# Mixture-of-experts routing in 16-bit floats, with the gates stored behind the feature rows

## The chip, the cores and the metric

The kernel runs on one core of one Trainium2 chip. The metric is the device time of one execution in microseconds (us), and the kernel before is given by the median of three runs: 1179.99 us (1179.2 to 1181.08). The profile is of one further execution, which took 1180.66 us; the span from its first to its last instruction is 1178.6 us.

Engines are named as the profile names them: PE (TensorE, matrix products into PSUM; PEld is its loading of the stationary operand), DVE (VectorE), ACT (ScalarE), POOL (GpSimd), SP (SyncE, which here only issues transfers).

## The reference

The reference is one block of a graph transformer on 1250 nodes with 768 features, all in fp32. Its last part, which the change touches, is a layer of eight experts of which each node uses two:

```python
xn = _layernorm(x)
x = x + gnn(xn, edges) + linear_attention(xn)
xt = _layernorm(x)                                # 1250 x 768
gate = xt @ Wg + bg                               # 1250 x 8
scores, idx = jax.lax.top_k(gate, 2)
h = gelu(einsum('td,edh->eth', xt, W1) + b1)      # 768 -> 384, each expert
y = einsum('eth,ehd->etd', h, W2) + b2            # 384 -> 768
comb = sum(one_hot(idx, 8) * scores[..., None])
out = x + einsum('te,etd->td', comb, y)
```

The score by which an expert's output is multiplied is the raw gate value of that node for that expert.

## The kernel before, in words

**Stages.** Until about 595 us the kernel builds the graph's adjacency and runs the two graph layers and the key side of the attention. From about 613 us it multiplies out the update weights, and from about 630 us a loop over ten tiles of 125 nodes (L768) makes the block's output and routes each tile. From about 937 us the experts run, one after the other; what they compute is added onto `out` in HBM.

**One tile of the loop.** `query(t + 1)` (L742 to 765) computes the next tile's attention queries: products `mm` on PE (L751), then on DVE L753 to L762, among them the normalisation `qy`, then transposes of `qy` on PE and their copy `qT` on ACT (L319 to L321, a helper called `turn`). Then 24 products `po` (L781) add the update of this tile, `xt` (the input rows, loaded by L772) gets its sums on DVE (L783, L786), four products `u` (L792) and their sums (L794) complete it. It is written to `out` (L797), normalised into `xl` (L800), and `xl` is written to a scratch matrix `xl_d` in HBM (L802). Transposed, it gives the gate: products `g` (L807), and `gate` on DVE (L810).

**Routing.** DVE ranks the eight gates of each node (L817 to L821), marks first and second choice (`kth`, L825) and their sum `sel`. Two products `g` at L830 count, for each expert, the nodes that chose it up to this one: a triangle of ones `tri` times `sel`, and a square of ones times the counts `cum` of the tiles before. From that each node's place in its expert's list follows (`at`, `two`, `both`; L833 to L845): a slot number and a row number. An expert's list has ten slots of 128 nodes, eight lists make NV = 80 slots. For each of the two choices, `hot` (L849) is a one-hot row of 128 by row number, `put` (L852) is a one-hot row of 80 by slot, once times the node's number and once times its gate, and the product `inv` (L854) of the two adds them into a 128 x 160 table in PSUM: node numbers in the first 80 columns, gates in the last 80. All these are fp32. After the last tile the two halves become `idx` (L858, L859) and `gs` (L861), and L866 to L895 work out which slots beyond the first three of an expert are in use; L867 uses `ones` and `cum` once more.

**Experts.** `gather` (L904) fetches three slots of an expert: for each, POOL issues an indirect load (L909) of 128 rows of `xl_d` by a column of `idx` into `xg`, which PE transposes into `px` (L912) and DVE copies to `xsT` (L915). `hidden` makes the first layer (L926), `give` the second (L938); DVE adds the bias (L941), ACT multiplies by a column of `gs` (L942), and POOL issues an indirect accumulating write to `out` (L943). The gather of the next expert is written between `hidden` and `give` of this one. A ninth round with one slot, `other` (L959), takes its slot and expert from values computed at run time.

**Order of the work.** Each engine runs its instructions in one fixed order. That order is not the source's: it is drawn up when the program is built, from the source's order and from what waits for what. In the trace, products of `query` for a later tile and `po` of the next tile stand on PE between the routing products of this tile. All loads and stores except the indirect ones go through SP's queue in SP's order; the indirect ones go through POOL's. Waits between engines are semaphores that are placed with the order.

Of the kernel before, what the change touches and what calls it, by code (L numbers as in the profile page):

```python
# [27 lines left out]
F32 = mybir.dt.float32  # L28
F16 = mybir.dt.float16
# [5 lines left out]
ALU = mybir.AluOpType  # L35
# [3 lines left out]
N, D = 1250, 768  # L39
PT, NT = 125, 10  # L40
# [3 lines left out]
NE, FF = 8, 384  # L44
# [9 lines left out]
NJ = -(-N // 128)  # L54
FIX = 3
NV = NE * NJ
# [13 lines left out]
def gps_block(ctx: ExitStack, tc: tile.TileContext, x, src, dst, norm_g, norm_b, W1, a_src1, a_dst1,  # L70
              b1, W2, a_src2, a_dst2, b2, Wu, bu, Wq, bq, Wk, bk, Wv, bv, Wo, bo, Wg, bg, fW1, fb1,
              fW2, fb2, out):
    nc = tc.nc
# [10 lines left out]
    dram = ctx.enter_context(tc.tile_pool(name="dram", bufs=1, space=bass.MemoryType.DRAM))  # L84
# [3 lines left out]
    def token_rows(t):  # L88
        return [(slice(0, 112), t), (slice(112, PT), t)]
# [40 lines left out]

    xl_d = dram.tile([N + 128, D], F32)

# [39 lines left out]
    rows = fl.tile([KC, 128], F32)  # L172
# [27 lines left out]
    with tc.tile_pool(name="eps", bufs=4, space=PSUM) as eps_p:  # L200
# [4 lines left out]
        for k in (1, 0):  # L205
            nc.vector.memset(ends[k][:, T:], float(NO_NODE))
            for r0, r1 in blocks128:
# [6 lines left out]
                if k == 1:  # L214
# [3 lines left out]
                                                   op0=ALU.is_lt, op1=ALU.mult)  # L218
# [21 lines left out]
    with tc.If(nc.values_load(odd[0:1, 0:1], min_val=0, max_val=1) > 0), ExitStack() as es:  # L240
# [9 lines left out]
        for j in range(NT):  # L250
# [21 lines left out]
            for g0 in range(0, NT, 4):  # L272
                n = min(4, NT - g0)
# [266 lines left out]
    with tc.tile_pool(name="wp", bufs=3) as wp, tc.tile_pool(name="rb", bufs=1) as rb:  # L540
# [20 lines left out]
        at = 2 * (C2 + 1)  # L561
# [123 lines left out]

    zero = fp.tile([128, D], F32)
    nc.gpsimd.memset(zero, 0.0)
    nc.sync.dma_start(xl_d[N:], zero)
    nc.sync.dma_start(out[N:], zero)
# [4 lines left out]
    gs = fp.tile([128, NV + 1], F32)  # L694
    fb1T = fp.tile([128, FC, NE], F32)
# [3 lines left out]
    with ExitStack() as rs:  # L699
# [6 lines left out]

        def numbers(shape, pattern, base, mult, name):
            t = rp.tile(shape, F32, name=name)
# [7 lines left out]
        nc.vector.tensor_scalar(upto, upto, 0.0, None, op0=ALU.is_ge)  # L716
        row128 = numbers([PT, 128], [[1, 128]], 0, 0, "row128")
        steps = numbers([128, NE, NJ - FIX], [[0, NE], [128, NJ - FIX]], 128 * FIX, 0, "steps")
        slot_row = numbers([PT, NV], [[1, NV]], 0, 0, "slot_row")
        base = numbers([PT, NE], [[128 * NJ, NE]], -1, 0, "base")  # L720
# [4 lines left out]
        nobody = numbers([128, 1], [[0, 1]], N + 1, 1, "nobody")  # L725
        ones = rp.tile([PT, 128], F32)
        nc.gpsimd.memset(ones, 1.0)
        tri = rp.tile([PT, 128], F32)
        nc.gpsimd.affine_select(tri, ones, pattern=[[1, 128]], compare_op=ALU.is_ge, fill=0.0,
                                base=0, channel_multiplier=-1)  # L730
        nc.gpsimd.tensor_copy(idx[:, NV:], nobody)
        nc.vector.tensor_scalar(idx[:, NV:], nobody, -1.0, None, op0=ALU.add)
        nc.gpsimd.memset(gs[:, NV:], 0.0)
        for f in range(FC):
# [3 lines left out]

        cum = rp.tile([PT, NT + 1, NE], F32)
        nc.vector.memset(cum[:, 0], 0.0)  # L740
        inv = g_p.tile([128, 2, NV], F32, name="inv", bufs=1)
        def query(t):  # L742
# [25 lines left out]
        for t in range(NT):  # L768
# [29 lines left out]

            xl = rl.tile([PT, D], F32, name="xl")
            normalise(xl, xt)  # L800
            for p, tt in token_rows(t):
                nc.sync.dma_start(xlr[p, tt], xl[p])  # L802
            xT = rl.tile([128, KC, PT], F32, name="xT")
            turn(xT, xl, u_p, "u", nc.scalar.copy)
            pg = g_p.tile([128, 2 * NV], F32, name="g")
            for c in range(KC):
                nc.tensor.matmul(pg[:PT, :NE], xT[:, c], Wg_sb[:, c], start=c == 0,  # L807
                                 stop=c == KC - 1)
            gate = rl.tile([PT, NE], F32, name="gate")
            nc.vector.tensor_add(gate, pg[:PT, :NE], bg_b)  # L810

            gt = rl.tile([PT, NE, NE], F32, name="gt")
# [9 lines left out]
            kth = rl.tile([PT, 2, NE], F32, name="kth")  # L822
            sel = rl.tile([PT, NE], F32, name="sel")
            for k in range(2):
# [8 lines left out]
            nc.vector.tensor_add(at, pp[:PT, :NE], base)  # L833
            two = rl.tile([PT, 2, 2, NE], F32, name="two")
            for i, a in enumerate((at, gate)):
                nc.vector.tensor_mul(two[:, i], kth, a[:, None, :].to_broadcast([PT, 2, NE]))
            both = rl.tile([PT, 2, 2], F32, name="both")
            nc.vector.tensor_reduce(both, two, AX.X, ALU.add)
            b_i = rl.tile([PT, 2], I32, name="b_i")
            nc.vector.tensor_copy(b_i, both[:, 0])  # L840
            s_i = rl.tile([PT, 2, 2], I32, name="s_i")
# [5 lines left out]
            for k in range(2):  # L847
                hot = rl.tile([PT, 128], F32, name="hot")
                nc.vector.tensor_scalar(hot, row128, s_f[:, 1, k:k + 1], None, op0=ALU.is_equal)  # L849
                put = rl.tile([PT, 2, NV], F32, name="put")  # L850
                for i, v in enumerate((node1[:, t:t + 1], both[:, 1, k:k + 1])):
                    nc.vector.tensor_scalar(put[:, i], slot_row, s_f[:, 0, k:k + 1], v,  # L852
                                            op0=ALU.is_equal, op1=ALU.mult)
                nc.tensor.matmul(inv.rearrange("p a s -> p (a s)"), hot,  # L854
                                 put.rearrange("p a s -> p (a s)"), start=k == 0 and t == 0,
                                 stop=k == 1 and t == NT - 1)
        free = rp.tile([128, NV], F32)
        nc.vector.tensor_scalar(free, inv[:, 0], 0.0, nobody, op0=ALU.is_equal, op1=ALU.mult)  # L858
        nc.vector.scalar_tensor_tensor(idx[:, :NV], inv[:, 0], -1.0, free, op0=ALU.add,  # L859
                                       op1=ALU.add)  # L860
        nc.vector.tensor_copy(gs[:, :NV], inv[:, 1])  # L861
        for e in range(1, 4):
# [40 lines left out]

    def gather(rows):  # L904

        xT = sp.tile([128, KC, FIX * 128], F32, name="xsT")
        for j, r in enumerate(rows):
# [9 lines left out]
        return xT  # L917

    def hidden(w, xT, n, bias):
# [26 lines left out]
    def fixed(e):  # L946
        return [(idx[:, v:v + 1], gs[:, v:v + 1]) for v in range(e * NJ, e * NJ + FIX)]

    xT = gather([r for r, _ in fixed(0)])
    for e in range(NE):  # L950
        hT = hidden(ring[e], xT, FIX, fb1T[:, :, e:e + 1])
        if e + 1 < NE:
            xT = gather([r for r, _ in fixed(e + 1)])
        for j, (rows, gates) in enumerate(fixed(e)):
            give(ring[e], hT, j, rows, gates)
        if e + 4 < NE:
            ring.append(expert(fW1[e + 4], fW2[e + 4], fb2[e + 4]))

    def other(k):  # L959

        ve = nc.values_load(v_row[0:1, k:k + 1], min_val=0, max_val=NV,
                            engines=[mybir.EngineType.DVE])
        ee = nc.values_load(e_row[0:1, k:k + 1], min_val=0, max_val=NE - 1,
                            engines=[mybir.EngineType.DVE, mybir.EngineType.SP])
        rows = sp.tile([128, 1], I32, name="rows")
        nc.vector.tensor_copy(rows, idx[:, bass.ds(ve, 1)])
        gates = sp.tile([128, 1], F32, name="gates")
        nc.vector.tensor_copy(gates, gs[:, bass.ds(ve, 1)])
# [4 lines left out]
        hT = hidden(w, gather([rows]), 1, bias)  # L973
        give(w, hT, 0, rows, gates)

# [40 lines left out]
```

## Time and profile before

| what | value |
|---|---|
| median of three runs | 1179.99 us |
| profiled execution, its span | 1180.66 us, 1178.6 us |
| PE busy | 1077.8 us (91%), 4583 instructions |
| DVE busy | 669.1 us (57%), 1366 instructions |
| ACT busy | 358.1 us (30%) |
| POOL busy | 76.3 us (6%) |
| granted PE clock, mean | 0.971 of full |
| g L830, 10 tiles | 40 records of 0.17 to 0.38 us |
| inv L854, 10 tiles | 40 records, 9.1 us busy |
| put L852 | 40 instructions, 12.6 us busy |

Busy time is the sum of the instructions of an engine. PE overlaps one product with the next and with the loads, so its busy share says little of how fast it works; what counts is the chain, which is followed back from the last instruction to what released each step. An fp32 product shows as two records on PE (x4 for two products). "Idle before" with an engine and a line names what a waiting instruction was released by. In lists by time, rows of one kind that follow each other are put together as x2, x4 and so on.

### The profile page before, as it was taken

To read this page: it belongs to the slowest core of one execution; us is meant where nothing else is said; L and a number is where in the kernel's file an instruction comes from. 1 tells how busy PE (TensorE), PEld (TensorE's weight loads), DVE (VectorE), ACT (ScalarE), POOL (GpSimd) and SP (SyncE) were. 2 spreads that over 40 slices of the span, in tenths; PEclk is the share of its full clock that TensorE was granted. 3 is DMA by queue.
4 is the path that set the end of the run, shared out by engine and by line. 5 is a ranking of instruction groups with operands and counts; after the bars stand their busy time and mean duration, and the time that the engine had idled before them with its cause. 6 is when DMAs were issued, how large, how long until landed. Compare 5 with 4: busy or idle time off the path is not lost.

```text
span 1178.6 us, 12106 instructions
## 1 busy us (share of the span) xinstructions
PE 1077.8 (91%) x4583; PEld 723.6 (61%) x4583; DVE 669.1 (57%) x1366; ACT 358.1 (30%) x527; POOL 76.3 (6%) x100
## 2 busy tenths in 40 slices
PE   2599998999999999988989999999999589999993
PEld 2586655578788878544545666666666356666652
DVE  6866666669696966687922555555555422222210
ACT  2131114373737373373712211111111011111111
POOL 1000000000000000000000000000000122322321
PEclk9999998999999999989989999999999789999997
DMA  5014000000000001000083111111123537777533
GB/s 156 27 51 163 16 25 1 1 1 1 1 1 1 1 1 53 1 0 1 1 319 103 40 40 40 40 40 40 39 65 106 191 91 188 200 209 219 121 56 54
DMA packets 33282, 79.62 MB, mean 68 GB/s; under 512 B 5258, under 2 KB 13020, under 8 KB 33208
## 3 DMA queue, kind: packets, MB, share of 16 engines
q1 hardware_dynamic: 27608, 59.02, 15.2%
q0 software_dynamic: 5600, 19.66, 8.4%
q8 instruction: 40, 0.66, 0.2%
q14 instruction: 34, 0.28, 0.1%
HBM read 60.37 MB, written 18.30 MB: 67 GB/s over the span
## 4 chain that ended last, share of the span: by engine, by line
PE 70%; DVE 20%; DMA 5%; issue 2%; ACT 2%; POOL 1%; DVEq 0%; SPq 0%; POOLq 0%; ACTq 0%
PE po L781 13%; PE ph L926 8%; PE py L938 7%; PE mm L430 7%; PE mm L607 7%; PE mm L751 7%; DVE scr L515 6%; DVE w L535 5%; DVE w L536 5%; PE ag L548 3%; PE ag L569 2%; PE u L792 2%; PE px L912 2%; PE mm L405 2%; DMA w<-in_L_gnn_Wu_dram 2%
## 5 line engine op out<-in xcount | busy, mean ns | idle before, releaser
L548 PE MATMUL ag<-kept,w 125*125 125x198 f32 x800 | 137.4, 333 | 5.1 <-DVE w L536 4.9
L548 PEld LDWEIGHTS ag<-kept,w 125*125 125x125 f32 x800 | 133.5, 188 | 9.0 <-DVE w L536 9.0
L926 PE MATMUL ph<-xsT,w 128*128 128x384 f32 (+1 forms) x324 | 100.6, 470 | 1.8 <-DVE xsT L915 1.8
L938 PE MATMUL py<-w,hT 128*128 128x384 f32 x300 | 100.6, 486 | 0.0
L430 PE MATMUL mm<-Wg,xnT 128*125 128x400 f32 x240 | 91.8, 520 | 1.0 <-DVE xnT L321 0.6
L607 PE MATMUL mm<-Wv_sb,xnT 128*125 128x384 f32 x240 | 85.7, 489 | 4.8 <-DVE kvacc L627 4.8
L535 DVE TENSOR_TENSOR w<-v,w 125x1250 f32<-125x1250 f32 x60 | 86.3, 1453 | 6.6 <-ACT w L533 5.9
L515 DVE CUSTOM_DVE_ANT_0 scr<-ss_row,mask 125x1250 bf16<-125x1250 f32 x60 | 87.2, 1453 | 0.5 <-ACT ss_row L506 0.2
L781 PE MATMUL po<-w,xnT 128*125 128x384 f32 x240 | 84.8, 496 | 2.6 <-DMA w<-in_L_gnn_Wu_dram 2.6
L536 DVE SCALAR_TENSOR_TENSOR w<-w,AT 125x1250 f32<-125x1250 f32 x60 | 86.4, 1455 | 0.4
L926 PEld LDWEIGHTS ph<-xsT,w 128*128 128x128 f32 x324 | 59.8, 193 | 41.4 <-DVE xsT L915 2.4
L607 PE MATMUL mm<-Wk_sb,xnT 128*125 128x384 f32 x240 | 84.4, 486 | 0.0
L534 ACT ACTIVATE v<-dn_row,sl 125x1250 f32<-125x1250 f32 x60 | 79.3, 1333 | 16.9 <-DVE w L535 16.4
L751 PE MATMUL mm<-w,xnT 128*125 128x384 f32 x240 | 84.2, 489 | 0.0
L915 DVE COPY xsT<-px 128x384 f32<-128x384 f32 x50 | 25.5, 552 | 99.2 <-PE px L912 77.3
L781 PE MATMUL po<-w,qT 128*125 128x384 f32 x240 | 80.8, 486 | 0.0
L938 PEld LDWEIGHTS py<-w,hT 128*128 128x128 f32 x300 | 55.3, 190 | 33.9
L941 DVE TENSOR_TENSOR ys<-py,wb 128x768 f32<-128x768 f32 x25 | 23.9, 958 | 74.0 <-PE py L938 45.5
L781 PEld LDWEIGHTS po<-w,xnT 128*125 128x125 f32 x240 | 44.2, 190 | 30.1 <-DMA w<-in_L_gnn_Wu_dram 2.8
L781 PEld LDWEIGHTS po<-w,qT 128*125 128x125 f32 x240 | 44.2, 188 | 29.4
L607 PEld LDWEIGHTS mm<-Wv_sb,xnT 128*125 128x125 f32 x240 | 42.4, 187 | 31.1 <-DVE kvacc L627 6.9
L751 PEld LDWEIGHTS mm<-w,xnT 128*125 128x125 f32 x240 | 43.6, 188 | 27.6 <-ACT qT L321 0.2
(274 smaller groups left out, 1415.6 us busy)
## 6 DMA issues: line engine op xcount, KB each, us to landing
w<-in_L_ffn_W_dram SPq DMA_DIRECT2D x18, 1152.0 KB
xt<-in_x_dram SPq DMA_DIRECT2D x20, 336.0 KB
wb<-in_L_ffn_b_dram SPq DMA_DIRECT2D x9, 384.0 KB
out_dram<-xt SPq DMA_DIRECT2D x10, 336.0 KB
xl_d<-xl SPq DMA_DIRECT2D x10, 336.0 KB
W_sb<-in_L_gnn_W_dram SPq DMA_DIRECT2D x1, 2304.0 KB
Wk_sb<-in_L_mix_Wk_dram SPq DMA_DIRECT2D x1, 2304.0 KB
Wv_sb<-in_L_mix_Wv_dram SPq DMA_DIRECT2D x1, 2304.0 KB
```

Source lines behind the costliest of these rows:

```text
L430: nc.tensor.matmul(ps[:PT, :2 * (CG + 2)], xnT[:, c, t * PT:(t + 1) * PT], Wg1[:, c, 2 * k:2 * k + 2].rearrange("p h c -> p (h c)"), start ...
L515: nc.vector.tensor_tensor_reduce(scr, ss_row, mask[:, t], 1.0, 0.0, ALU.mult, ALU.max, top[:, t:t + 1])
L534: nc.scalar.activation(v, dn_row, AF.Exp, bias=sl[:, st:st + 1])
L535: nc.vector.tensor_tensor(w, v, w, op=ALU.max)
L536: nc.vector.scalar_tensor_tensor(w, w, 2.0, AT[:, st, :N], op0=ALU.min, op1=ALU.mult)
L548: nc.tensor.matmul(ag[:, t // 2, o:o + CG], w[:, t * PT:(t + 1) * PT], gw[:, st, hd], start=st == 0 and t % 2 == 0, stop=st == NT - 1, ski ...
L607: nc.tensor.matmul(ps[:PT, :384], xnT[:, c, t * PT:(t + 1) * PT], w[:, c, half], start=c == 0, stop=c == KC - 1)
L751: nc.tensor.matmul(ps[:PT, :384], xnT[:, c, tk], Wq_sb[:, c, half], start=c == 0, stop=c == KC - 1)
L781: nc.tensor.matmul(po[k][:, :384], l, r[:, k * 384:(k + 1) * 384], start=i == 0, stop=i == len(parts) - 1)
L915: nc.vector.tensor_copy(xT[:, 3 * a:3 * a + 3, j * 128:(j + 1) * 128], px[:, a, :384].rearrange("p (b n) -> p b n", b=3))
L926: nc.tensor.matmul(ph[:, :n * 128], w[0][:, o:o + 128], xT[:, c, :n * 128], start=c == 0, stop=c == KC - 1)
L938: nc.tensor.matmul(py[:, k, :384], hT[:, f, j * 128:(j + 1) * 128], w[:, o:o + 384], start=f == 0, stop=f == FC - 1)
```

## The change

Two things are changed.

First, types. `row128`, `slot_row`, `ones`, `tri`, `cum`, `sel`, `hot` and `put` become 16-bit floats. Their values are 0, 1, slot and row numbers, node numbers and counts up to 1250, all whole numbers that a 16-bit float holds exactly up to 2048. Products still add up in fp32 in PSUM.

Second, the gates take another way. A row of `xl_d` is 776 instead of 768 numbers long: behind the features stand the node's eight gates. `gate` is now the end of the tile `xl`, and two more transfers per tile (112 and 13 rows of 32 bytes) write it. The gates' half of `two`, `both`, `put` and `inv` goes, and with it `gs`. A gather brings the eight gates along, and one more DVE copy per slot takes the expert's column out of `xg` into `gates`; for the computed slot the column is given by a register.

The diff, cut to its core:

```diff
-    xl_d = dram.tile([N + 128, D], F32)
+    xl_d = dram.tile([N + 128, D + NE], F32)
...
-        row128 = numbers([PT, 128], [[1, 128]], 0, 0, "row128")
+        row128 = numbers([PT, 128], [[1, 128]], 0, 0, "row128", F16)
-        slot_row = numbers([PT, NV], [[1, NV]], 0, 0, "slot_row")
+        slot_row = numbers([PT, NV], [[1, NV]], 0, 0, "slot_row", F16)
-        ones = rp.tile([PT, 128], F32)
+        ones = rp.tile([PT, 128], F16)
-        tri = rp.tile([PT, 128], F32)
+        tri = rp.tile([PT, 128], F16)
...
-        cum = rp.tile([PT, NT + 1, NE], F32)
+        cum = rp.tile([PT, NT + 1, NE], F16)
-        inv = g_p.tile([128, 2, NV], F32, name="inv", bufs=1)
+        inv = g_p.tile([128, NV], F32, name="inv", bufs=1)
...
-            xl = rl.tile([PT, D], F32, name="xl")
-            normalise(xl, xt)
+            xl = rl.tile([PT, D + NE], F32, name="xl")
+            normalise(xl[:, :D], xt)
             for p, tt in token_rows(t):
-                nc.sync.dma_start(xlr[p, tt], xl[p])
+                nc.sync.dma_start(xlr[p, tt, :D], xl[p, :D])
...
-            gate = rl.tile([PT, NE], F32, name="gate")
+            gate = xl[:, D:]
             nc.vector.tensor_add(gate, pg[:PT, :NE], bg_b)
+            for p, tt in token_rows(t):
+                nc.sync.dma_start(xlr[p, tt, D:], gate[p])
...
-            sel = rl.tile([PT, NE], F32, name="sel")
+            sel = rl.tile([PT, NE], F16, name="sel")
...
-            two = rl.tile([PT, 2, 2, NE], F32, name="two")
-            for i, a in enumerate((at, gate)):
-                nc.vector.tensor_mul(two[:, i], kth, a[:, None, :].to_broadcast([PT, 2, NE]))
+            two = rl.tile([PT, 2, NE], F32, name="two")
+            nc.vector.tensor_mul(two, kth, at[:, None, :].to_broadcast([PT, 2, NE]))
...
-                hot = rl.tile([PT, 128], F32, name="hot")
+                hot = rl.tile([PT, 128], F16, name="hot")
                 nc.vector.tensor_scalar(hot, row128, s_f[:, 1, k:k + 1], None, op0=ALU.is_equal)
-                put = rl.tile([PT, 2, NV], F32, name="put")
-                for i, v in enumerate((node1[:, t:t + 1], both[:, 1, k:k + 1])):
-                    nc.vector.tensor_scalar(put[:, i], slot_row, s_f[:, 0, k:k + 1], v,
-                                            op0=ALU.is_equal, op1=ALU.mult)
+                put = rl.tile([PT, NV], F16, name="put")
+                nc.vector.tensor_scalar(put, slot_row, s_f[:, 0, k:k + 1], node1[:, t:t + 1],
+                                        op0=ALU.is_equal, op1=ALU.mult)
...
-        nc.vector.tensor_copy(gs[:, :NV], inv[:, 1])
...
-            xg = sp.tile([128, D], F32, name="xg", bufs=3)
+            xg = sp.tile([128, D + NE], F32, name="xg", bufs=3)
...
+            at = slice(D + e, D + e + 1) if isinstance(e, int) else bass.ds(e + D, 1)
+            nc.vector.tensor_copy(gates[:, j:j + 1], xg[:, at])
```

`give` then multiplies by a column of `gates`. `hidden` is renamed `inner` and is otherwise the same; `zero`, which fills the rows of `xl_d` behind the last node, is as wide as the new rows.

More of the change, by code (lines that the diff above doesn't have):

```diff
@@ L684, in gps_block @@
             nc.scalar.copy(Wo_sb[:, c, half], ps[:, :384])
-    zero = fp.tile([128, D], F32)
+    zero = fp.tile([128, D + NE], F32)
     nc.gpsimd.memset(zero, 0.0)
     nc.sync.dma_start(xl_d[N:], zero)
-    nc.sync.dma_start(out[N:], zero)
+    nc.sync.dma_start(out[N:], zero[:, :D])
     ring = [expert(fW1[0], fW2[0], fb2[0])]
@@ L693, in gps_block @@
     idx = fp.tile([128, NV + 1], I32)
-    gs = fp.tile([128, NV + 1], F32)
     fb1T = fp.tile([128, FC, NE], F32)
@@ L705, in gps_block, with numbers @@
         u_p = rs.enter_context(tc.tile_pool(name="u_p", bufs=2, space=PSUM))
-        def numbers(shape, pattern, base, mult, name):
-            t = rp.tile(shape, F32, name=name)
+        def numbers(shape, pattern, base, mult, name, dt=F32):
+            t = rp.tile(shape, dt, name=name)
             nc.gpsimd.iota(t, pattern=pattern, base=base, channel_multiplier=mult,
@@ L732, in gps_block @@
         nc.vector.tensor_scalar(idx[:, NV:], nobody, -1.0, None, op0=ALU.add)
-        nc.gpsimd.memset(gs[:, NV:], 0.0)
         for f in range(FC):
@@ L833, in gps_block @@
             nc.vector.tensor_add(at, pp[:PT, :NE], base)
-            two = rl.tile([PT, 2, 2, NE], F32, name="two")
-            for i, a in enumerate((at, gate)):
-                nc.vector.tensor_mul(two[:, i], kth, a[:, None, :].to_broadcast([PT, 2, NE]))
-            both = rl.tile([PT, 2, 2], F32, name="both")
+            two = rl.tile([PT, 2, NE], F32, name="two")
+            nc.vector.tensor_mul(two, kth, at[:, None, :].to_broadcast([PT, 2, NE]))
+            both = rl.tile([PT, 2], F32, name="both")
             nc.vector.tensor_reduce(both, two, AX.X, ALU.add)
             b_i = rl.tile([PT, 2], I32, name="b_i")
-            nc.vector.tensor_copy(b_i, both[:, 0])
+            nc.vector.tensor_copy(b_i, both)
             s_i = rl.tile([PT, 2, 2], I32, name="s_i")
@@ L847, in gps_block @@
             for k in range(2):
-                hot = rl.tile([PT, 128], F32, name="hot")
+                hot = rl.tile([PT, 128], F16, name="hot")
                 nc.vector.tensor_scalar(hot, row128, s_f[:, 1, k:k + 1], None, op0=ALU.is_equal)
-                put = rl.tile([PT, 2, NV], F32, name="put")
-                for i, v in enumerate((node1[:, t:t + 1], both[:, 1, k:k + 1])):
-                    nc.vector.tensor_scalar(put[:, i], slot_row, s_f[:, 0, k:k + 1], v,
-                                            op0=ALU.is_equal, op1=ALU.mult)
-                nc.tensor.matmul(inv.rearrange("p a s -> p (a s)"), hot,
-                                 put.rearrange("p a s -> p (a s)"), start=k == 0 and t == 0,
+                put = rl.tile([PT, NV], F16, name="put")
+                nc.vector.tensor_scalar(put, slot_row, s_f[:, 0, k:k + 1], node1[:, t:t + 1],
+                                        op0=ALU.is_equal, op1=ALU.mult)
+                nc.tensor.matmul(inv, hot, put, start=k == 0 and t == 0,
                                  stop=k == 1 and t == NT - 1)
         free = rp.tile([128, NV], F32)
-        nc.vector.tensor_scalar(free, inv[:, 0], 0.0, nobody, op0=ALU.is_equal, op1=ALU.mult)
-        nc.vector.scalar_tensor_tensor(idx[:, :NV], inv[:, 0], -1.0, free, op0=ALU.add,
-                                       op1=ALU.add)
-        nc.vector.tensor_copy(gs[:, :NV], inv[:, 1])
+        nc.vector.tensor_scalar(free, inv, 0.0, nobody, op0=ALU.is_equal, op1=ALU.mult)
+        nc.vector.scalar_tensor_tensor(idx[:, :NV], inv, -1.0, free, op0=ALU.add, op1=ALU.add)
         for e in range(1, 4):
@@ L902, in gps_block, with gather @@
     y_p = ctx.enter_context(tc.tile_pool(name="y_p", bufs=2, space=PSUM))
-    def gather(rows):
+    def gather(rows, e):
         xT = sp.tile([128, KC, FIX * 128], F32, name="xsT")
+        gates = sp.tile([128, FIX], F32, name="gates")
         for j, r in enumerate(rows):
-            xg = sp.tile([128, D], F32, name="xg", bufs=3)
+            xg = sp.tile([128, D + NE], F32, name="xg", bufs=3)
             nc.gpsimd.indirect_dma_start(xg, None, xl_d, bass.IndirectOffsetOnAxis(r, 0))
@@ L916, in gather, with inner @@
                                       px[:, a, :384].rearrange("p (b n) -> p b n", b=3))
-        return xT
-    def hidden(w, xT, n, bias):
+            at = slice(D + e, D + e + 1) if isinstance(e, int) else bass.ds(e + D, 1)
+            nc.vector.tensor_copy(gates[:, j:j + 1], xg[:, at])
+        return xT, gates
+    def inner(w, xT, n, bias):
         hT = sp.tile([128, FC, FIX * 128], F32, name="hT")
@@ L946, in fixed @@
     def fixed(e):
-        return [(idx[:, v:v + 1], gs[:, v:v + 1]) for v in range(e * NJ, e * NJ + FIX)]
-    xT = gather([r for r, _ in fixed(0)])
+        return [idx[:, v:v + 1] for v in range(e * NJ, e * NJ + FIX)]
+    ahead = gather(fixed(0), 0)
     for e in range(NE):
-        hT = hidden(ring[e], xT, FIX, fb1T[:, :, e:e + 1])
+        xT, gates = ahead
+        hT = inner(ring[e], xT, FIX, fb1T[:, :, e:e + 1])
         if e + 1 < NE:
-            xT = gather([r for r, _ in fixed(e + 1)])
-        for j, (rows, gates) in enumerate(fixed(e)):
-            give(ring[e], hT, j, rows, gates)
+            ahead = gather(fixed(e + 1), e + 1)
+        for j, rows in enumerate(fixed(e)):
+            give(ring[e], hT, j, rows, gates[:, j:j + 1])
         if e + 4 < NE:
@@ L966, in other @@
         nc.vector.tensor_copy(rows, idx[:, bass.ds(ve, 1)])
-        gates = sp.tile([128, 1], F32, name="gates")
-        nc.vector.tensor_copy(gates, gs[:, bass.ds(ve, 1)])
         bias = sp.tile([128, FC, 1], F32, name="bias")
@@ L972, in other @@
                    fW2[bass.ds(ee, 1)].rearrange("o d f -> (o d) f"), fb2[bass.ds(ee, 1)])
-        hT = hidden(w, gather([rows]), 1, bias)
-        give(w, hT, 0, rows, gates)
+        xT, gates = gather([rows], ee)
+        hT = inner(w, xT, 1, bias)
+        give(w, hT, 0, rows, gates[:, :1])
     def others(k):
```

## The prediction

> **What bounds the kernel now.** I read the page first (1180.66 us for the profiled execution, 1178.6 us of it span), then the chain in order of time over one steady token tile, then the timeline of VectorE and SyncE in that tile, then the chain of the last tile. The routing work sits in the loop over ten token tiles (roughly 672 to 937 us). In it the chain is TensorE without a gap:
>
> ```profile
> 851.97 0.35 PE g L830 x4
> 852.31 2.68 PE po L781 x8
> 854.99 0.67 PE inv L854 x4
> 855.66 4.52 PE po L781 x14
> 860.18 0.65 PE mm L319 x6
> 860.83 7.10 PE po L781 x22
> ```
>
> Columns: start, length, engine, tile, line, count. The next tile's g L830 comes 29.53 us later (881.84 - 852.31 between the same po groups in the whole chain), and table rows by stage show TensorE busy in all of it. So what is cut from TensorE here shortens the tile, unless VectorE then sets the pace. VectorE is close to that (start, length, engine, line, operation, tiles):
>
> ```profile
> 852.35 0.17 DVE L833 TENSOR_TENSOR at<-g,base 125x8 f32<-125x8 f32 x1 [0.25 <-PE g L830]
> ...
> 854.09 0.32 DVE L852 TENSOR_SCALAR put<-slot_row,s_f,both 125x80 f32<-125x80 f32 x1
> 854.33 0.28 DVE L849 TENSOR_SCALAR hot<-row,s_f 125x128 f32<-125x128 f32 x1
> ...
> 854.75 0.31 DVE L852 TENSOR_SCALAR put<-slot_row,s_f,both 125x80 f32<-125x80 f32 x1
> 854.98 0.95 DVE L756 SCALAR_TENSOR_TENSOR qy<-qy,qe 125x768 f32<-125x768 f32 x1
> ...
> 858.95 0.96 DVE L762 TENSOR_TENSOR qy<-qy,den 125x768 f32<-125x768 f32 x1
> ```
>
> From `at` to the end of L762 (859.91) VectorE has no pause, and the transposes of qy (L319) start on TensorE at 860.01: their weight load started at 859.97, so VectorE is 0.04 us from being the one that ends last. Both must be shortened for the tile to shrink. After the last tile nothing covers the routing:
>
> ```profile
> 930.49 1.04 PE g L830 x4
> ...
> 931.77 0.61 PE g L867 x2
> ...
> 933.79 0.47 DVE put L852 x2
> ...
> 934.30 1.57 PE inv L854 x4
> ...
> 935.90 0.30 DVE free L858
> ...
> 937.47 4.06 DMA xg<-xl_d,idx
> ```
>
> Here every step delays the first gather and so all eight experts, which then keep TensorE busy for 190.87 of the 190.90 us from 949.1 to 1140.
>
> **What the Trainium skill says.** "FP8 and Floating Point Precision", section TensorE Precision Notes: true fp32 takes four passes through the array. The trace agrees: an fp32 product of 384 columns is two records that take 0.65 us of the chain (L751 x2), 1.7 ns a column. "TensorE: Matmul & The Clock Gate", section on weight-path perf modes: a load of 128 weights that aren't fp32 can be about twice as fast. The trace has fp32 loads of 186 to 192 ns and bf16 ones of 138 ns with 125 columns, none with 128 and 16 bits. "VectorE: DVE Perf Modes", perf-mode tier table: tensor_scalar from SBUF runs at 4 elements a cycle in 16 bits, 2 in fp32; no row before shows the 16-bit form here. "DMA: Bandwidth & Descriptors", Specifications: writes under 512 B are read-modify-write; no such write to HBM is in this stage of the trace before.
>
> **The change, part by part.**
>
> *TensorE, a steady tile.* The fp32 pairs become single records, 16-bit, of 8 and 80 columns. The nearest row is the 16-bit product with a fresh weight load at full clock: eight ec L350 take 0.47 us, ten pm L465 take 0.58 us of the chain, so 0.058 us each. g L830: 2 x 0.058 = 0.12 instead of 0.35, saves 0.23. inv L854: 0.12 instead of 0.67 (of which about 0.1 us is waiting for the second put), saves 0.55. Sum 0.78 us. Bounds: 0.85 if the 128-column load is quicker, 0.70 if a change of type costs some 0.04 us at each group.
>
> *VectorE, a steady tile.* Two puts go, 0.23 us each by their starts (854.09 to 854.33): 0.46. g L830 ends 0.23 earlier. hot and put in 16 bits: 128 columns at 4 instead of 2 a cycle is 32 cycles, 33 ns, an estimate by the VectorE page; the starts are 0.2 us apart at any size here, so 0 to 0.11 us in four instructions; I take 0.05. The gate product L836 goes too (0.08 us between starts), outside this stretch. Sum 0.74, and with the 0.04 in hand VectorE allows 0.78. The tile thus shrinks by 0.77 us, and both engines stay level. Nine tiles: **6.9 us**.
>
> *The last tile*, at half clock, with cold 16-bit products at 0.107 us apart (ten pm L465 in 1.07 us) and 315 ns from start to end (longest of that row). g L830: 0.04 + 0.107 + 0.315 = 0.46 instead of 1.06 to the start of `at`: 0.60. g L867, for which VectorE waits before it goes on: 0.36 instead of 0.64: 0.28. Two puts: 0.46. From the last put (934.90) to `free` (935.90) 1.0 us becomes about 0.5, because begin, late, mine and place (until 935.38) are then last: 0.50. Sum 1.84 us. The copy of gs comes after idx, and saves nothing there.
>
> *The first gather.* It is issued 0.99 us after idx is written (936.24 + 0.24). The named releaser is the transpose L894, which moves up as well. Rows grow from 3072 to 3104 bytes: 1% of 4.06 us at least, 0.4 us if odd row starts cost 10%; I take 0.1. If the wider buffer falls on a tile that the second L894 still reads, up to 0.75 us more. Net of the tail: **1.7 us**.
>
> *Gate writes*, two per tile of 112 and 13 rows with 32 bytes each. Nobody on an engine waits for them but the gathers. SyncE's row of the tile:
>
> ```profile
> 846.26 0.76 SPq L802 DMA_DIRECT2D xl_d<-xl  x2
> 847.13 0.92 SPq L772 DMA_DIRECT2D xt<-in_x_dram  x2
> ```
>
> The gate is ready at 849.49. Placed after L772, its writes cost nothing: SyncE is then idle until 871.84. Placed before it, in source order, the loads of the next xt start at 849.5 + 0.8 = 850.3 instead of 847.13; their traffic ended by 851 before (DMA share 0.17 from 850 to 851, zero after), so it would end at about 854 with the small writes. L783 reads xt at 855.85, now some 0.75 earlier, 855.1: hidden with 1 us to spare, on VectorE before L757, L759 and the qy chain. Without that cover each microsecond late is one per tile. The last tile's gate is ready at 928.79; SyncE issued its last weight load at 925.56 and the DMA share is 0.05 from 932 to 933, so the writes land by about 933 even behind those weights. The gather would go at 937.47 - 1.84 = 935.6: 2.6 us of cover.
>
> *Expert phase.* 24 copies of one column (gates to xg), about 0.15 us each by the old copy L968, 3.7 us of VectorE, which is busy 42 of 191 us there and waits mostly for py. They read xg after the gather, as the transposes do, so they add no earlier wait; a buffer of xg comes free about 1 us later, against 25 us until its next use. The copy of the computed slot moves from before its gather to after it, ahead of nothing that ends last: the end is the row of accumulating writes to out from 1146 on. Cost 0. Iotas, memsets and the zero store of 3104-byte rows lie behind the weight loads at 594 to 613 us: 0.
>
> **Sum:** 6.9 + 1.7 = 8.6 us; the profiled execution goes from 1180.66 to 1172.1, the span to 1170.0, and the median of three runs, 1179.99, to **1171.4**.
>
> **Rivals.** (A) *The order of instructions is drawn anew.* The trace shows that each engine's order is not the source's: products of later tiles stand between routing's. Eight po records (2.68 us) now cover VectorE's stretch from g L830 to the second put (2.9 us). Shorter routing may leave six (1.93 us) against about 2.35: 0.4 us of waiting per tile, 3.6 in nine. For: cover and stretch are matched to 0.2 us today. Against: the stretch shrinks by as much as a po pair. Time 1180.0 - 5.0 = 1175.0. (B) *Hidden anyway:* if qy's chain starts from something that the change doesn't shorten (exp L755, done by 852.9), only the tail is won: 1178.3. Against: L756 follows the last put at once, and exp was done 2 us before. (C) *Slower: the gate write stands before the next xt load in SyncE's queue and makes xt late.* VectorE stops before L783, and with it qy, its transposes and po. It needs xt to land after 855.1; to lose the gain it must land 0.95 us later than that on all nine tiles, and with 1.4 us later the kernel takes 1180.0 + 12.6 - 8.6 = 1184.0. For: source order puts it there. Against: my estimate of 854. (D) *The change doesn't do what it says:* if one 16-bit product took as long as its fp32 pair, g L830 would save nothing, and inv only the width and the wait for the second put, about 0.2 per tile, with 1 us at the end: 1177.2. Against: the 0.058 us rows.
>
> **How the numbers follow.** My forecast (1169.5 to 1173.5) 0.60; A and D (1173.5 to 1177.6) 0.22; B 0.08, within 0.2% (2.4 us, about what a measurement of this kernel can tell from no change); C 0.10. The range 1168.8 to 1177.6 holds the first two, 0.82; its low end is 0.85 a tile and 2.5 us at the end, with something over. Faster 0.82, same 0.08, slower 0.10.
>
> **What would show it.** Right: tile period near 28.76 us; g L830 and inv L854 at two records each and about 0.12 us of the chain; no TensorE idle before L854 or L319; inv to first gather shorter, with idx near 1.8 us sooner after the last gate; experts unchanged. Wrong: VectorE idle before L783 until an xt landing (C), TensorE waiting for put (A) or for qy L762, the first gather waiting for a gate write, or 16-bit records more than 0.1 us apart at full clock (D).

## The result, and the profile after

The changed kernel takes 1167.35 us (median of 6 runs, 1160.77 to 1169.57) against 1180.09 us (6 runs, 1176.61 to 1182.83) for the kernel before: ratio 0.9892, 95% interval 0.9872 to 0.9912. That is faster, as forecast, but by 12.7 us instead of 8.6, and 1.45 us below the low end of the range. Two repetitions gave 0.9899 (0.9879 to 0.9918) and 0.9912 (0.9893 to 0.9932).

The profiled execution after took 1167.08 us, its span 1165.0 us. Between landmarks that both traces have, in us:

| stage | before | after | difference |
|---|---|---|---|
| start to the first po product | 612.97 | 610.79 | -2.18 |
| to the first count product g (L830, now L831) | 62.18 | 61.92 | -0.26 |
| to the ninth one: eight tiles | 234.46 | 228.21 | -6.25 |
| to the tenth one | 20.88 | 19.83 | -1.05 |
| to the first gather | 6.98 | 4.48 | -2.50 |
| to the first ph product | 11.66 | 11.72 | +0.06 |
| to the eighth expert's first py product | 190.95 | 190.66 | -0.29 |
| to the last accumulating write to `out` | 26.59 | 25.70 | -0.89 |
| to the end | 11.94 | 11.71 | -0.23 |

So 9.8 us come from the loop and the steps behind it (the rows of the eight tiles, the tenth count product and the first gather), and 3.8 us from stages in which the change does nothing or nearly nothing. Both parts need an explanation.

**A steady tile.** The chain of waits of the kernel after (start us, length us, engine, line, count), the same stretch as in the prediction:

```profile
844.82 0.03 PE g L831 x2
844.85 2.04 PE po L780 x6
846.89 0.04 PE inv L853
846.93 0.72 PE po L780 x2
847.65 0.04 PE inv L853
847.68 4.59 PE po L780 x14
852.27 0.64 PE mm L319 x6
```

From the start of g to the end of the mm group there were 8.87 us before (0.35 + 2.68 + 0.67 + 4.52 + 0.65), and there are 8.09 now. TensorE still has no gap, and the period is 28.77 us instead of 29.53. The two `inv` products have come apart: the first now stands after six po records (three products), as rival A said, but it doesn't wait there, and the second stands two records later. VectorE in the same tile (timeline: start, length, engine, line, operation, tiles):

```profile
844.89 0.17 DVE L834 TENSOR_TENSOR at<-g,base 125x8 f32<-125x8 f32 x1
...
846.73 0.30 DVE L851 TENSOR_SCALAR put<-slot_row,s_f,node 125x80 f16<-125x80 f16 x1
...
850.91 0.96 DVE L761 TENSOR_TENSOR qy<-qy,den 125x768 f32<-125x768 f32 x1
```

It ends at 851.87, and the weight load of the transposes of qy starts 0.05 us later, as before (859.91 and 859.97). But the product behind that load follows at 852.11, 0.19 us after it, where it followed within 0.05 us before: TensorE is still busy with po then. So VectorE shrank by a little more than TensorE, and has some 0.14 us in hand.

**Behind the last tile.** The chain after:

```profile
920.76 0.21 PE g L831 x2
...
920.99 0.18 DVE at L834
...
921.21 0.18 PE g L863
...
923.13 0.22 DVE put L851
...
923.40 0.24 PE inv L853
...
923.66 0.30 DVE free L856
...
925.24 4.12 DMA xg<-xl_d,idx
```

What the products gain is larger than the prediction had it: g to `at` takes 0.23 us instead of 1.06. The weight loads (PEld) say why. Before, the loads of `tri` and `ones` belong to their fp32 product and start with it, when `sel` is there; after, they are instructions of their own. First before, then after:

```profile
930.49 0.50 PEld L830 LDWEIGHTS g<-sel,tri 125*128 125x128 f32 x2 [2.00 <-DVE sel L826]
```

```profile
918.50 0.29 PEld L831 LDWEIGHTS <-tri 125*128 125x128 f16 x1
...
920.78 0.10 PEld L863 LDWEIGHTS <-ones 125*128 125x128 f16 x1
```

`tri` is loaded 2.26 us before its product at 920.76, and the `ones` of the total at 920.78, 0.43 us before theirs at 921.21. The Trainium skill, "TensorE: Matmul & The Clock Gate", section Step-by-step: what each phase is for, says that TensorE pulls weight loads ahead of products that are under way. This trace agrees for the 16-bit products; the fp32 loads of `tri` and of the total's `ones` in the kernel before wait with theirs (930.49 and 931.77).

**The gates' writes.** SyncE's queue after:

```profile
842.37 0.75 SPq L811 DMA_DIRECT2D xl_d<-xl  x2
843.23 0.76 SPq L771 DMA_DIRECT2D xt<-in_x_dram  x2
```

They stand ahead of the next load of `xt`, the order that rival C needs. The packets of that load end at 845.75, and VectorE adds `bu_b` to `xt` at 847.80.

### The profile page after: what moved, and what is told of

The parts are those of the page before. It is cut to its first block, busy times and chain, and to the rows that moved or that the text cites. A ratio compares the mean times of both kernels' runs of the same rounds, so it can differ in the third digit from the quotient of the medians.

```text
span 1165.0 us, 12068 instructions
## 1 busy us (share of the span) xinstructions
PE 1066.3 (92%) x4542; PEld 712.8 (61%) x4542; DVE 665.0 (57%) x1359; ACT 358.1 (31%) x527; POOL 76.5 (7%) x99
## 4 chain that ended last, share of the span: by engine, by line
PE 70%; DVE 20%; DMA 3%; issue 2%; ACT 2%; POOL 0%; DVEq 0%; SPq 0%; POOLq 0%; ACTq 0%
PE po L780 14%; PE ph L925 9%; PE py L937 7%; PE mm L430 7%; PE mm L607 7%; PE mm L750 7%; DVE scr L515 6%; DVE w L535 5%; DVE w L536 5%; PE ag L548 3%; PE ag L569 2%; PE u L791 2%; PE mm L405 2%; PE px L909 2%; DMA w<-in_L_gnn_Wu_dram 2%
```

## The experiments

**Theory S:** the change acts in the loop and behind its last tile, by the sum of its parts; the rest of the difference is chance of an execution. **Theory P:** it also shifts the rest of the program, so that stages with unchanged code become shorter. Later came theory F, a form of P. All ratios are to the kernel before.

**1. The kernel before once more** (no edit).

> The kernel before, unchanged, against itself. Theory S (the change acts only in the routing loop and in the stretch from the last count product to the first gather; the rest of the 13.6 us between the two profiles, 2.2 us before the first po product and about 1.4 us after the first expert product, is chance of an execution, such as where TensorE's half-clock windows fall): ratio 1.000 within 0.002, and the start of the first po product moves by 1 to 3 us between executions of one and the same program (612.97 in the profile before). Theory P (the change also moves the rest of the program, for instance by where its code or buffers lie): the first po product is again at 613.0 within 0.5 us.

Measured: 1178.93 us (14 runs), ratio 0.9993 (0.9984 to 1.0002). Eight tiles 234.44 us, first count product to first gather 262.32 us as in the first profile; the first po product at 612.14 instead of 612.97, and from the eighth expert's first py to the end 39.1 us (before: 38.5). The first po product moved by 0.83 us, which lies between what S (1 to 3) and P (at most 0.5) had. The loop repeats within 0.02 us; the stages before and behind it repeat within about 1 us only.

**2. The kernel after once more** (no edit), twice.

> The changed kernel again. Theory S: from the first count product (675.15 before, 672.71 after) to the first gather 252.5 us within 0.3 (262.3 before), start of the first po product anywhere from 609 to 615 us, time 1168 to 1172 us, ratio 0.990 to 0.993. Theory P: first po product again near 610.8 us, ratio 0.987 to 0.9895.

> The kernel after, once more, for another profile of the stages that the change doesn't touch. Theory S: the first po product starts where its clock lets it, anywhere from 609 to 613 us, as in the kernel before; from the first count product to the first gather 252.6 us as before within 0.2; the last gather to the end as chance has it. Theory P: the first po product below 612 us again and the last four accumulating writes within 20 us, as in both profiles of this kernel so far. Either: 1167.2 us (1166 to 1169).

Measured: 1167.16 us (5 runs) and 1167.81 us (4 runs), with the ratios given above. First count product to first gather 252.64 and 252.51 us (252.53 in the first profile, 262.3 before): 9.7 to 9.8 us of gain. It isn't quite fixed: the padded form of the same kernel in 7. has 253.1, because its ninth tile takes 20.39 us. Of the ratios one lies in the range that S had, one between the two ranges. First po product at 611.90 and 610.65; from the eighth expert's py to the end 36.6 and 37.1 us, again below the 38.5 and 39.1 of before. So the gain at the end isn't a single execution's, and S in its plain form doesn't cover it.

**3. Counts only in 16 bits.**

```diff
-        ones = rp.tile([PT, 128], F32)
+        ones = rp.tile([PT, 128], F16)
-        tri = rp.tile([PT, 128], F32)
+        tri = rp.tile([PT, 128], F16)
-        cum = rp.tile([PT, NT + 1, NE], F32)
+        cum = rp.tile([PT, NT + 1, NE], F16)
-            sel = rl.tile([PT, NE], F32, name="sel")
+            sel = rl.tile([PT, NE], F16, name="sel")
```

> Of the change only ones, tri, cum and sel in 16 bits; lists and gates as before. Theory S: the tile is 0.23 us shorter (29.3 us), eight tiles 1.9 us; from the last count product to the first gather 0.83 + 0.44 = 1.3 us less (5.7 instead of 6.98); together with the first tile about 3.4 us, 1176.6 us. Rival (VectorE sets the pace, so a shorter product alone brings nothing): eight tiles 234.5 us as before, 1178.7 us.

Measured: 1174.04 us (6 runs), ratio 0.9958 (0.9942 to 0.9974). Period 29.22 us, 0.32 less; from the last count product to the first gather 5.73 us, 1.25 less. In its chain the two g products take 0.03 us of a tile, and the po group behind them is as long as before:

```profile
846.47 0.03 PE g L830 x2
846.50 2.68 PE po L781 x8
```

So g gives 0.32 us a tile, not the 0.23 that the prediction had. VectorE doesn't hold this gain back: with g done earlier, it starts earlier too. From the first count product to the first gather it is 4.0 us less; the time fell by more than the expectation had (1176.6), and what lies beyond the 4.0 lies outside this stretch.

**4. The gates' new way only, everything in fp32** (the kernel after with F32 for each F16).

> Of the change only the gates' new way (stored behind the features, no gate half of two, both, put and inv, no gs); all in fp32. Theory S: inv, 80 columns wide, is bound by its four loads of 0.11 us, 0.2 us less per tile in all; VectorE gets 0.46 us shorter, which then doesn't count: eight tiles 1.6 us less, the end 0.7 to 1.0 us less, 1177.2 us. Rival (VectorE sets the pace): 0.46 us per tile, 3.7 us in eight, 1175.3 us. If the gate writes or the 25 copies cost something, it shows as more than 1179 us.

Measured: 1177.99 us (22 runs), ratio 0.9990 (0.9981 to 0.9999). Period 29.43, 0.11 less (0.2 expected); tail 6.36 us, 0.62 less (0.7 to 1.0 expected). With one put less for each choice, the two fp32 `inv` products come apart, two po records between them:

```profile
850.67 0.32 PE inv L853 x2
...
851.67 0.18 PE inv L853 x2
```

`inv` takes 0.50 us instead of 0.67, but the po groups around it take 7.28 instead of 7.20 (2.04, 0.69 and 4.55): half the columns and two puts less give only 0.11 us a tile as long as the products are fp32.

**5. The gates' new way and the lists in 16 bits, counts in fp32** (the kernel after with F32 for `ones`, `tri`, `cum`, `sel`).

> The gates' new way, and row128, slot_row, hot and put in 16 bits; the triangle, ones, cum and sel stay in fp32. Steady tile: counts alone gave 0.32 us a tile and everything gives 0.77, so if the parts add up this gives 0.45, a period of 29.09 us, of which 0.11 is the gates' way. If a tile saves only where TensorE and VectorE shrink together, the parts don't add up: this gives then under 0.35 or over 0.55. From the last count product to the first gather: 6.98 - 2.50 + 1.25 = 5.73 us if the parts add up there too. Theory S (the change acts in the loop and behind its last tile only): 8 x 0.45 + 0.1 + 1.25 + 0.5 in the last steps = 5.5 us, 1174.1 us. Theory P (16-bit or wider buffers also move the rest of the program): 1.5 to 3 us below that.

Measured: 1173.53 us (6 runs), ratio 0.9961 (0.9946 to 0.9976). Period 29.07, 0.47 less (0.45 expected); tail 5.74 us, 1.24 less (1.25 expected). The parts add up: 0.32 + 0.47 = 0.79 against 0.77 in a tile, 1.25 + 1.24 = 2.49 against 2.50 behind the last. Of the lists' share, 0.11 and 0.62 are the gates' way, the rest is 16 bits.

**6. More small writes ahead of `xt`.** Two, then four more pairs of writes of the gates per tile, to a scratch matrix (here four):

```diff
+    again = dram.tile([4, N, NE], F32)
...
+            for r in range(4):
+                for p, tt in token_rows(t):
+                    nc.sync.dma_start(again[r].rearrange("(t p) d -> p t d", p=PT)[p, tt], gate[p])
```

> The kernel after, with each tile's gates written two more times, to a scratch matrix, by the same kind of transfer and ahead of the next load of xt in SyncE's queue. A pair of writes holds that queue for 0.86 us (842.37 to 843.23), so xt's load starts 1.72 us later and its traffic ends at 847.47 instead of 845.75 on the time axis of the profile after. Theory L: xt is needed where VectorE adds bu_b to it, at 847.80, so this is still hidden: period 28.77 us, 1167.2 us. Theory W: the wait for xt stands in VectorE's queue ahead of the step of qy before it, at 846.92, so that work is held too: 0.55 us a tile and more by what a landing takes to be seen, period 29.3 to 29.6 us, nine tiles, 1172 to 1175 us.

> The same with four more writes per tile: xt's traffic ends at 849.2. Theory L: 1.4 us late per tile, period 30.2 us, 1167.2 + 12.6 = 1180 us. Theory W: 2.3 us late per tile and somewhat more, period 31.1 to 31.4 us, 1167.2 + 21 to 24 = 1188 to 1191 us. If neither holds and the load of xt has cover that I don't see, 1167 us.

Measured: 1166.97 us (4 runs, ratio 0.9907, 0.9884 to 0.9929) and 1168.82 us (4 runs, 0.9930, 0.9908 to 0.9952). The period is 28.76 us in both, so W held for neither, and L, whose number came out for two writes, failed for four: the load does go late, and nothing waits. SyncE and VectorE with four:

```profile
842.08 3.46 SPq L815 DMA_DIRECT2D again<-xl  x8
845.58 0.78 SPq L772 DMA_DIRECT2D xt<-in_x_dram  x2
```

```profile
849.95 0.95 DVE L783 TENSOR_TENSOR xt<-xt,kept 125x768 f32<-125x768 f32 x1
```

The order was drawn anew with the later load in it: the addition to `xt` stood behind the first of qy's five steps in the kernel after; with two writes more it stands behind the third (848.03, its packets having ended at 845.72), with four behind all five. With four the packets end at 848.07, and `xt` is used at 849.95. Where it stands costs nothing, because the sums of po come more than 7 us later (VectorE is idle 7.54 us before L785 in the kernel after). So rival C had a cover that its price left out. What a late `xt` costs in the old order isn't shown, because the order moved with it.

**7. The end of the kernel: theory F.** In the packets of the last four accumulating writes one thing stands out: in all three profiles whose routing products are fp32 (before, its repetition, 4.) a transfer of the program's own instructions, one packet of 16 KB, starts 0.1 to 2.0 us after the first packet of the second of them, whose packets then take 3.82 to 4.03 us. In the profiles with 16-bit products they take 2.67 to 3.23 us. Six of these have no such packet there, but three (3., 5. and 8.) have one too, which starts 2.3 to 2.8 us after the first packet of the write, and their write takes 3.08 to 3.23 us. So a fetch inside this write isn't enough for the long time. The DMA view of that write, before and in 3.:

```profile
q0 software_dynamic: 144, 0.39, 74.9%
q8 instruction: 1, 0.02, 1.4%
```

```profile
q0 software_dynamic: 144, 0.39, 86.1%
q8 instruction: 1, 0.02, 2.0%
```

The Trainium skill, "Runtime: NRT & Kernel Launch", section Instruction fetch mechanics, says that instructions come in 16 KiB blocks of 256, their cost mostly hidden; the packet size agrees. By the listing of its program the changed kernel has 41 more weight loads, one for each of its 41 16-bit products (in the trace 20 of `hot`, 10 of `tri`, 11 of `ones`). Two kernels move TensorE's program without executing anything more, by transposes in a branch that these inputs don't take: 41 in the kernel before, and 215 in the kernel after, which with its 41 loads make one block.

```diff
         tr_p = es.enter_context(tc.tile_pool(name="tr_p", bufs=2, space=PSUM))
+        tr = tr_p.tile([PT, 4, PT], F32)
+        for _ in range(41):
+            nc.tensor.transpose(tr[:8, 0, :8], ident[:8, :8], ident[:8, :8])
```

> The kernel before with 41 small transposes in the branch for odd edge lists, which these inputs don't take: nothing more is executed, but TensorE's later instructions stand 41 places later in its program, as they do in the kernel after, where each of 41 16-bit products has a weight load of its own. Theory F: TensorE's program is fetched in 16 KB pieces at fixed places of it, and in the kernel before one such fetch falls into the second of the last four accumulating writes to out (its packets take 3.93 us there, 4.03 in the other profile of this kernel, 3.82 in gates32, and 2.7 to 3.2 in every kernel with 16-bit products). Then no fetch lies in that write here and it takes 2.7 to 3.2 us; from the last expert's last py stage on the kernel is about 0.9 us shorter: 1178.7 us by the median of before. Theory N (chance, or the 16-bit work itself): the write takes 3.8 to 4.0 us again with a fetch in it, 1179.6 us.

> The kernel after with 215 such transposes in the branch that isn't taken[...]. Theory F: the fetches stand in TensorE's program where they stand in the kernel before, and the second of the last four writes takes 3.8 to 4.0 us instead of 2.8 to 3.0: 1168.1 us. Theory N: 2.7 to 3.2 us, 1167.2 us. In both: eight tiles 228.2 us, last count product to first gather 4.5 us.

Measured, one execution each: 1179.95 and 1168.84 us, which decides nothing at this size. In the trace of the first the fetch has left the second write, which takes 3.24 us, just above the expected range:

```profile
q0 software_dynamic: 144, 0.39, 90.7%
```

From the eighth expert's first py to the end it is 37.8 us, against 38.5 and 39.1: 0.7 to 1.3 less. In the second, no fetch lies in that write, which takes 2.96 us (the nearest ones start 12.6 us before it and 2.2 us after its end), so this half of F's forecast fell. What stands: in the one execution taken, 41 places that aren't executed moved the fetch away, and the write was 0.7 to 0.8 us shorter. That the fetch is what lengthens the write isn't shown. A rule by which its place in the write decides would fit the second writes, early and long against late and short, but not the third ones: in every profile a fetch begins in the last part of the third write, and these take 3.03 to 3.80 us, the longest in the second repetition of after.

From the eighth expert's first py to the end, all nine profiles with 16-bit products take 36.1 to 37.5 us, the three with fp32 products 38.5 to 39.1, and the padded kernel before 37.8. So the shorter end goes with the 16-bit products, also with those of 3. or 5. alone; why stays open.

**8. TensorE kept busy behind the last tile.**

```diff
+        for _ in range(12):
+            nc.tensor.transpose(pr[:NV, :128], free, ident)
...
+            if isinstance(e, int) and e == 0 and j < 2:
+                pd = h_p.tile([128, 512], F32, name="ph")
+                for _ in range(5):
+                    nc.tensor.transpose(pd[:, :128], xg[:, :128], ident)
```

> The kernel after with 22 more transposes that nobody reads, where TensorE waits after the last tile: 12 of free behind the two of L890, and five each behind the first and second px of the first expert. What it tells: whether the half clock behind the last tile comes from TensorE having little to do, and what it costs. Theory H (it does): the first px takes 1.51 us (six transposes at half clock) and becomes about 0.8, and the first ph products run at full clock; the stage from the first gather to the first ph, 11.7 us, becomes 10.5 to 11.5, and from there to the last expert's py, 190.7, becomes 188 to 189.5: 1163 to 1166 us. Theory I (the clock goes its own way): the same stages as in the kernel after, 1167.2 us, or some 0.5 us more if the added transposes delay px.

Measured: 1164.52 us (5 runs, 1163.99 to 1167.41), ratio 0.9884 (0.9863 to 0.9905). From the first gather to the eighth expert's first py it is 199.6 us instead of 202.2 to 202.4, so 2.7 us less, by theory H. The second px in the kernel after, then the added transposes and both first px here:

```profile
932.13 1.51 PE L909 MATMUL px<-ident,xg 128*128 128x128 f32 x6 [1.16 <-DVE gates L915]
```

```profile
926.89 2.78 PE L893 MATMUL g<-ident,free 128*80 128x128 f32 x12 [0.37 <-DVE e_row L891]
929.88 1.23 PE L911 MATMUL px<-ident,xg 128*128 128x128 f32 x6 [0.21 <-issue]
...
933.01 0.85 PE L911 MATMUL px<-ident,xg 128*128 128x128 f32 x6 [0.44 <-issue]
```

The first px takes 1.23 us and the second 0.85, instead of 1.51 each, and the first real ph product comes 10.7 us after the gather instead of 11.7. The granted clock agrees: the half-clock stretch that begins in the ninth tile lasts 23.9 us in all three profiles of the kernel after (916.7 to 940.5 in the first) and 13.7 us here (917.0 to 930.7). The half clock there is the price of a TensorE that waits, and products that nobody reads take it away. This kernel has the lowest median of those run; its lead of 2.7 us over the kernel after rests on the trace's stages, since the two were not timed side by side.

**The clock before the loop.** The 2.2 us ahead of the first po product come from two stretches, near 165 and near 195 us. By stretch (the third number from the end is the granted clock), the first of them in the second repetition of after, and in the padded kernel after (before: 0.59):

```profile
165.00:169.00 4.00, 3.91 (x12) 2.31 (x13) 3.05 (x9) 0.00 (x0) 0.00 (x0) 1.00 0.23 87
```

```profile
164.00:168.00 4.00, 4.00 (x8) 2.06 (x9) 2.75 (x8) 0.00 (x0) 0.00 (x0) 0.60 0.21 79
```

In this stretch stand the 24 records of the products `mm` from `Wg` that begin near 165 us. Over all traces they take, from the first start to the last, either 8.85 us (after, both repetitions, the kernels of 4., 5. and 8., and the one with four writes) or 10.2 to 10.5 us (before, its repetition, its padded form, 3., the one with two writes, and the padded form of after). In the six slow ones a half-clock stretch of 3.41 us begins within 0.7 us of the group's start, in the seven others none does. The Trainium skill, "TensorE: Matmul & The Clock Gate", section What's actually happening, has it that the clock follows activity in free-running windows of 3.4 us. The traces agree: within one trace all half-clock stretches begin on one grid of 3.413 us, and last multiples of it (but for the one that the end of the span cuts off), and the grid lies elsewhere in the span of every execution, also in two of the same kernel. Kernels with the whole change are on both sides, so these 1.5 us of the difference between the first two profiles are best put down to the draw of an execution. That the program has a share in it isn't ruled out: the two profiles of before and that of its padded form are all slow here, the three of after all fast.

## Why the prediction was right and wrong

**What bounds the kernel: right.** TensorE without a gap, VectorE close behind; both still hold after.

**A steady tile: right in its sum, by luck, since two errors cancel.** Forecast 0.77 to 0.78 us and a period near 28.76; measured 0.77 and 28.77. But g gave 0.32 instead of 0.23: the pair takes 0.03 us of the chain, not 0.12. And `inv` gave about 0.45 instead of 0.55: its two products take 0.08 us, less than assumed, but the po groups around them take 7.35 us instead of 7.20. The 0.058 us rows that I priced with were products that follow each other; a lone 16-bit product or pair among fp32 products takes less of the chain. The po products behind g pay nothing for it (2.68 us in 3., as before). Those around `inv` do, but half of that, 0.08 us, they also pay in 4., where fp32 `inv` products stand at the same places. VectorE's part shrank by 0.89 us, from the start of g to the end of the normalisation of qy (L762, now L761), where I had 0.74; each `hot` takes 0.25 us instead of 0.28, which the estimate of 33 ns had.

**The failed steps: "the last tile, at half clock", 1.84 us (1.7 net), and the stages put at 0.** The mechanism behind the last tile was right, its size wasn't: it measured 2.50 us. By its terms: g to `at` 0.83 (1.06 to 0.23) instead of 0.60; the wait for the total, as the time from `at` to `s_f`, 0.44 (1.71 to 1.27) instead of 0.28; from `s_f` to the end of the last put 0.55 (1.64 to 1.09) instead of 0.46; from there to `free` 0.69 (1.00 to 0.31) instead of 0.50. The first two are the loads: I priced a product at half clock with its load (0.107 us) and with the longest record of its row (315 ns), where the load was long done and `at` starts 0.21 us after the second product does (920.78 to 920.99). The last is an order that I took as given: I had `begin`, `late`, `mine` and `place` stand ahead of `free`; now `mine` and `place` stand behind it (923.88 and 924.24), and `free` starts as soon as the second `inv` is there. The first gather, for whose longer rows I had 0.1 us, takes 4.12 us instead of 4.06, where the repetitions of both kernels spread from 4.03 to 4.08.

**The ninth tile** is 1.05 us shorter by its landmarks where g and `inv` together give 0.77; it ends at half clock (4.5 us of it before, 4.1 in the first profile after). The repetitions of after spread there from 19.82 to 19.95 us, and the others with the change in full go up to 20.49, where the half clock takes 7.0 us of it.

**What was costed at nothing and was nothing:** the gates' copies (0.15 us each; one stands on the chain, with 0.07 us, and the stage from gather to ph grew by 0.06 us), the expert phase (190.66 against 190.95 us), the set-up. The last tile's gate writes were issued at 919.08 and had landed at 920.42, 4.8 us before the gather, where I had 2.6.

**What was put at 0 and wasn't:** "the end is the row of accumulating writes", cost 0. From the last expert stages on it became 0.9 to 1.1 us shorter in the first profile, and shorter in every profile with 16-bit products. Experiment 7 points to a fetch of TensorE's instructions, moved by the loads that the 16-bit products add, but kernels that keep such a fetch in the second write end as early. The cause stays open.

**The account.** 9.7 to 9.8 us between the first count product and the first gather and about 1 at the end make 10.8 us. Nothing that the change shortens stands ahead of the first count product; the stage before it takes 61.0 to 62.9 us over all traces, with the change and without. The three measurements say 12.7, 12.4 and 10.8 us, each with an interval of about 2.3 us to either side. Whether what lies beyond 10.8 us is more than scatter isn't settled. Between the two first profiles the spans differ by 13.6 us, 5.0 more than the forecast: 2.2 lie ahead of the first po product, 1.1 at the end, 0.8 behind the last tile, 0.4 in the nine tiles, and 0.5 in the stages between. The range's low end (11.2 us of gain) held the mechanism's 9.8 us; it left no room for stages that I took as fixed.

**The rivals.** A's order came true in half and its wait didn't: six po records (2.04 us, not 1.93) stand ahead of the first `inv`, which needs the first put alone, and the second has two records more; VectorE's stretch from the start of g to the end of the last put shrank from 3.09 to 2.21 us. B fell: the gain is in the tile. C fell: its order was there, but `xt` had 2 us to spare instead of 1, and three to five times the writes changed no steady tile. D fell at the 0.03 us of g.

## What to carry to other kernels

Where a small fp32 product stands on the critical path behind a late streaming operand and its stationary operand is a constant, 16 bits can be worth more than the columns say: here the load became an instruction of its own and was done before the operand came. Price such a product from a lone record, not from a row of equal ones, and look at what the product behind it then takes. And where a forecast leaves stages out as unchanged, their scatter between repeated executions (here 1 to 2 us of 1180) still belongs into its range.

## What the hardware showed that I had not expected

- A 16-bit pair of products with 8 columns takes 0.03 us of the chain at full clock, where the fp32 pair takes 0.35. VectorE's next step starts 0.20 us after the second product does, at full and at half clock alike (with fp32, after its last record: 0.29 and 0.40).
- An accumulating write of 128 rows of 3072 bytes takes 2.67 to 4.03 us by its packets, the second of the last four alone. The three longest have a 16 KB fetch of instructions 0.1 to 2.0 us after their first packet; three with one 2.3 to 2.8 us after it take 3.08 to 3.23.
- 22 transposes without a reader, put where TensorE waits, cut a half-clock stretch from 23.9 to 13.7 us and made the kernel 2.7 us shorter from the first gather on, in the one profile taken.
